# Layer 3's FFN: the last unit's parts between the attention's first steps in the first call, and in two halves of the tokens in the second

## The chip, the cores and the metric

The kernel runs on one core of a Trainium2 chip. The core has five engines with queues of their own: TensorE (PE, with its weight loads as PEld), VectorE (DVE), ScalarE (ACT), GpSimd (POOL) and SyncE (SP, which issues DMAs here). The metric is the device time of one execution in microseconds; the time before is the median of three runs, 2940.64 us.

## The reference

A macaron network of four layers on x, which has 2048 rows of 128. Each layer is an FFN with weight 0.5, an attention, and the same FFN again; each gets the normed x:

```
x = x + 0.5 * L3_ffn(layernorm(x))
x = x +       L3_attn(layernorm(x))
x = x + 0.5 * L3_ffn(layernorm(x))
```

For this case only layer 3 matters. Its attention is dense (16 heads of 8, rotary q and k). Its "FFN" is itself a small transformer of depth 2. One of its layers computes, with h = x whose upper 64 features are shifted by one token:

```
q, k, v = split(h @ wqkv);  q, k normed, scaled, rotated
o = attention in windows of 64 tokens over this and the window before
x = x + o @ wo
h = shift(x);  h = (h - mean) / sqrt(var + 1e-5) * lg + lb
a, g = split(h @ w1 + b1);  x = x + (a * gelu(g)) @ w2 + b2
```

## The kernel before, in words

All arithmetic is in 32-bit floats. x stays in SBUF as 16 tiles of 128 tokens; a *sequence* is four tiles (512 tokens), and there are four. `yT` holds a sequence's normed input with the features on the partitions. The file computes the layers one after the other; at its end stand `l3_ffn(w3, "l3f", True)`, `l3_attn()` and `l3_ffn(w3, "l3g", False)`.

**`l3_ffn` (line 1534 on).** A *unit* is one of the two inner layers for one sequence: eight units, each of four steps (a step is 128 tokens). A loop over steps runs six stages with lags: `project` (p_qk, pv), `to_features`, `weights`, `exponentials`, `turn_weights`, `with_values` (which copies a step's result into `oT`). The rest of a unit is a chain of *parts* over 512 tokens that is placed between later steps by the list `parts`:

- `attended`: pz = oT by wo (four calls), added to yT (L1702), and the shifted copy h (ACT L1551, DVE L1560)
- `mean`: pm, then h - pm (L1711) and its square on ACT
- `variance`: pvar, copied to rs (L1723), and an inverse root of ten small operations on POOL (L184 to L194)
- `spread` and `normed`: dg (L1731), pb = a matmul of dg, h scaled by it (L1741)
- `hidden` for three chunks (128, 128 and 85 columns): two calls into the bank pair pag, gelu on ACT (ge), hh on DVE (L1754)
- `close_unit`: pz2 from hh by w2 (three calls), added to yT (L1766)
- `leave`: transposes back (pt_z), x updated (L1774), and then, in the first call, `leave_normed`, or in the second, the DMA of the sequence to the output

For the last unit no later step is left to stand beside these parts: the loop runs on to `n_steps + 14` with nothing else in it.

**`leave_normed`** makes a *chain* of parts for the next layer: statistics of x on DVE (L202 to L190), scaling to y (L214), the turn to `yT` (pt_y on PE, L241 on ACT). A chain's part runs at a `tick()`, which the loops call after each stage; a tick that is told it is busy, or that has run one part with matmuls, leaves further such parts for later.

**`l3_attn`, `dense_attention` (line 720 on).** Four sequences of four units with four key tiles, in two halves: 128 half-steps. A half-step is scores (pk), the maxima of five steps ahead (pq on PE, L752 on DVE), the exponential on ACT (L787), and the product with the values (po). Before the first pk stand, for sequence 0, the four projections with their evacuations (L1499 and L1505), the sum on POOL (L1506), the marked keys km, the values, and ten maxima.

**What sets the order.** Matmuls, and the operations of ACT that are marked so, stand in the order in which the program emits them. DVE, POOL and SP are ordered by a scheduler among what is emitted. Semaphores come from the use of tiles: a tile of a pool waits until the one that had its place is read.

**PSUM.** There are eight banks of 512 columns. `l3_ffn` has `d=3` pairs (p_qk, pt_qk, ps, pt, pag) and `m=2` single banks for the rest. The attention has `MIX`: one pair k (pk), two pairs q (pq), one bank o (po), one bank m for all else:

```
MIX = dict(k=1, q=2, o=1, m=1)
```

Of the kernel before, what the change touches and what calls it, by code (L numbers as in the profile page):

```python
# [25 lines left out]
ALU = mybir.AluOpType  # L26
AX = mybir.AxisListType

P = 128
# [74 lines left out]
def tile_macaron(ctx, tc, x_in, const_in, vec_in, w0_in, ws_in, ws3_in, w2f_in, w3_in, out):  # L104
# [17 lines left out]
    def bank(tag, name):  # L122
        n = 2 if tag in "kqd" else 1
        return psum["pool"].tile([P, n * 512], F32, tag=tag, name=name, bufs=psum["bufs"][tag])
# [595 lines left out]
    def dense_attention(sb, prepare, finish, wo, masked, tiles=None):  # L720
# [119 lines left out]
        for u, (b, j) in enumerate(units):  # L840
            n = TB * u
            later.setdefault((n - 1, 0), []).append(lambda u=u: queries(u))
            later.setdefault((n + 5, 1), []).append(lambda u=u: end(u))
            if j == 3:
                later.setdefault((n + 6, 1), []).append(lambda b=b: output(b))
                later.setdefault((n + 7, 1), []).append(lambda b=b: project(b))
            if j == 0:
                for at, f in prepare(b, seq(b)["vh"], seq(b)):
                    if b or at >= -LEAD:
                        later.setdefault((n + math.floor(at), int(at % 1 * 2)), []).append(f)  # L850
                    else:
                        f()

        for n in range(-LEAD, n_steps + 5):
            for half in range(2):
# [675 lines left out]

    def l3_ffn(w3, tag, first):
        with pool(tag) as sb, banks(tag + "ps", d=3, m=2):
            units = [(l, b) for l in range(2) for b in range(B)]
            n_steps = TB * len(units)
# [4 lines left out]
                return W3(w3, f"{name}{l}")  # L1542

            def tmp(name):
                return sb.tile([P, S], F32, tag="tmp", name=name, bufs=4)

            def act(*args, **kw):
                tc.keep_in_program_order(nc.scalar.activation(*args, **kw))  # L1548
# [1 line left out]
            def act_copy(dst, src):  # L1550
                tc.keep_in_program_order(nc.scalar.copy(dst, src))  # L1551

            def pair(name):
                return bank("d", name)

            def shift(dst, src):

                act_copy(dst[0:64], src[0:64])
                nc.gpsimd.memset(dst[64:128, 0:1], 0.0)
                nc.vector.tensor_copy(dst[64:128, 1:S], src[64:128, 0 : S - 1])  # L1560

            def norm_unit(u):
                l, b = units[u]
# [113 lines left out]
            def with_values(step):  # L1677
                u, t = step // TB, step % TB
                st = s_state[step]
                PT = st["PT"]  # L1680
                po = bank("m", "po3")
                for fc in range(4):
                    for w, v in enumerate((st["vb"], st["v"])):
                        for r in range(2):
                            h = 2 * fc + r
                            mm_in_order(
                                po[64 * r : 64 * r + 64, fc * P + w * 64 : fc * P + w * 64 + 64],
                                v[:, ts(h, 64)], PT[:, r * 4 + fc, ts(w, 64)],
                            )
                if t == 0:  # L1690
                    u_state[u]["oT"] = sb.tile([P, 4, S], F32, tag="oT", name="oT")
                nc.vector.tensor_copy(u_state[u]["oT"][:, :, ts(t, P)], po.rearrange("p (c n) -> p c n", n=P))
                s_state.pop(step - 1, None)

            def attended(u):
                l, b = units[u]
                oT = u_state[u]["oT"]
                pz = bank("m", "pz")
                for fc in range(4):
                    mm_in_order(pz, W(l, "wo").rearrange("p (c n) -> p c n", n=D)[:, fc, :], oT[:, fc, :], fc == 0, fc == 3)  # L1700
                z = yT[:, b, :]
                nc.vector.tensor_add(z, pz, z)  # L1702
                h2 = sb.tile([P, S], F32, tag="h2", name="h2", bufs=2)
                shift(h2, z)
                u_state[u]["h2"] = h2

            def mean(u):
                h2 = u_state[u]["h2"]
                pm = bank("m", "pm")
                mm_in_order(pm, onesm, h2)  # L1710
                nc.vector.tensor_sub(h2, h2, pm)  # L1711
                sq = tmp("sq2")
                act(sq, h2, AF.Square)
                u_state[u]["sq"] = sq

            def variance(u):

                sq = u_state[u].pop("sq")
                pv = bank("m", "pvar")
                for t in range(TB):  # L1720
                    mm_in_order(pv[:, 2 * t : 2 * t + 2], sq[:, ts(t, P)], onesm[:, 0:2])
                rs = sb.tile([P, TB], F32, tag="rs", name="rs", bufs=2)
                nc.vector.tensor_copy(rs, pv[:, : 2 * TB].rearrange("p (t i) -> p t i", i=2)[:, :, 0])  # L1723
                inverse_root(sb, rs, rs, "ir4", ALU.add, 1e-5, nc.gpsimd)
                u_state[u]["rs"] = rs

            def spread(u):

                rs = u_state[u].pop("rs")
                dg = tmp("dg")  # L1730
                nc.vector.scalar_tensor_tensor(  # L1731
                    dg.rearrange("p (t n) -> p t n", n=P), rows(ident, TB), float(D), bcast(rs, P), ALU.mult, ALU.mult
                )
                u_state[u]["dg"] = dg

            def normed(u):
                l, b = units[u]
                h2 = u_state[u]["h2"]
                pb = bank("m", "pb3")
                mm_in_order(pb, onesm, u_state[u].pop("dg"))  # L1740
                nc.vector.scalar_tensor_tensor(h2, h2, W(l, "lg"), pb, ALU.mult, ALU.mult)  # L1741

            def hidden(u, c):
                l, b = units[u]
                at, n = HCH[c]
                h2, w1 = u_state[u]["h2"], W(l, "w1")
                if c == 0:
                    u_state[u]["hh"] = sb.tile([P, 3, S], F32, tag="hh", name="hh")
                p = pair("pag")
                mm_in_order(p[:n, 0:512], w1[:, HID + at : HID + at + n], h2)  # L1750
                mm_in_order(p[:n, 512:1024], w1[:, at : at + n], h2)
                ge = tmp("ge")
                act(ge[:n, :], p[:n, 0:512], AF.Gelu, bias=W(l, "b1g")[:n, c : c + 1])
                nc.vector.scalar_tensor_tensor(  # L1754
                    u_state[u]["hh"][:n, c, :], p[:n, 512:1024], W(l, "b1a")[:n, c : c + 1], ge[:n, :], ALU.add, ALU.mult
                )

            def close_unit(u):
                l, b = units[u]
                hh = u_state[u]["hh"]  # L1760
                w2 = W(l, "w2").rearrange("p (c n) -> p c n", n=D)
                z = yT[:, b, :]
                pz = bank("m", "pz2")
                for c, (_, n) in enumerate(HCH):
                    mm_in_order(pz, w2[:n, c, :], hh[:n, c, :], c == 0, c == 2)
                nc.vector.scalar_tensor_tensor(z, pz, W(l, "b2"), z, ALU.add, ALU.add)  # L1766
                del u_state[u]

            def leave(b):
                pt = bank("m", "pt_z")  # L1770
                for t in range(TB):
                    transpose_in_order(pt[:, ts(t, P)], yT[:, b, ts(t, P)])
                xb = x[:, ts(b, TB), :].rearrange("p t d -> p (t d)")
                nc.vector.scalar_tensor_tensor(xb, pt, 0.5, xb, ALU.mult, ALU.add)  # L1774
                if first:
                    leave_normed(b, chain(b), 3)
                else:
                    nc.sync.dma_start(out[:, ts(b, TB), :], x[:, ts(b, TB), :])

            if first:  # L1780
                for l in range(2):
# [14 lines left out]
                (lambda u: hidden(u, 0), 12, 5), (lambda u: hidden(u, 1), 13, 0), (lambda u: hidden(u, 2), 13, 0),  # L1796
                (close_unit, 13, 4), (lambda u: leave(units[u][1]) if units[u][0] else None, 14, 0),
            ]
            later = {}
            for u in range(len(units)):  # L1800
                for f, after, place in parts:
                    later.setdefault((u * TB + after, place), []).append((f, u))
                later.setdefault((u * TB - 2, 0), []).append((norm_unit, u))
                later.setdefault((u * TB - 1, 0), []).append((open_unit, u))
            for n in range(-2, n_steps + 14):
                for place, (part, lag) in enumerate((
                    (project, 0), (to_features, 2), (exponentials, 4), (weights, 3), (turn_weights, 5), (with_values, 6)
                )):
                    for f, u in later.pop((n, place), ()):
                        f(u)  # L1810
                    if 0 <= n - lag < n_steps:
                        part(n - lag)
                    tick()
            assert not later, later


    with pool("ws") as wp:
# [9 lines left out]
        with pool("l2x") as l2x:  # L1827
# [14 lines left out]
                l2_attn(v4s)  # L1842
                finish_chains()
            l2_ffn("l2g")
    l3_ffn(w3, "l3f", True)
    l3_attn()
    l3_ffn(w3, "l3g", False)

# [142 lines left out]
```

## Time and profile before

| what | value |
|---|---|
| median of three runs | 2940.64 us (2930.02 to 2940.65) |
| profiled execution, own time | 2936.27 us |
| its span, first to last instruction | 2934.6 us |
| busy PE, DVE, ACT, POOL | 78%, 62%, 42%, 31% of the span |
| mean granted clock of PE | 0.864 |
| HBM traffic | 28 GB/s over the span |

The page's shares are means over the whole kernel, of which layer 3 is some 1235 us (from 1700 to the end). A stage's limit is read in that stage: from the busy time in a stretch, from the timeline (start, duration, engine, line, operation, what goes out and in; in brackets the idle time before it and what ended it), and from the granted clock in a stretch.

### The profile page before, as it was taken

The page shows a single profiled execution, that of the slowest core. Times are in us where ns is not written, and L with a number is a line of the kernel's source. Part 1 is how long each engine was busy: PE and PEld are TensorE (multiplying, and loading weights), DVE is VectorE, ACT ScalarE, POOL GpSimd, SP SyncE. Part 2 cuts the span into 40 slices and gives each one's busy share as a digit, 9 for nine tenths or more (in the row PEclk, how much of TensorE's full clock was granted, in tenths as well). Part 3 has the DMA queues.
Part 4 walks back from the last instruction along what each step waited for, and adds up shares of the span by engine and source line. Part 5 has one row for each costly group of instructions (what it writes and reads, how often), then busy time and mean ns, then how long its engine had stood idle before and what let it go on. Part 6 is the DMA issues. An engine that isn't in the chain of part 4 may idle for free.

```text
span 2934.6 us, 46900 instructions
## 1 busy us (share of the span) xinstructions
PE 2274.4 (78%) x17558; PEld 1179.6 (40%) x17558; DVE 1808.6 (62%) x4776; ACT 1246.5 (42%) x2682; POOL 913.9 (31%) x1700
## 2 busy tenths in 40 slices
PE   4277528888678998958577678988689999689987
PEld 2145213333333333338456545555322222355553
DVE  4656476676576676454564477777356564777763
ACT  3044303433332433314232266776224444467763
POOL 1012012332122222202322387775200000677661
PEclk8588758999887999768777789999779999899998
DMA  3042010000000000008105410000000000100000
GB/s 133 0 152 81 0 58 1 1 1 1 1 1 1 1 1 4 4 7 290 36 13 189 143 30 21 21 21 12 1 1 1 1 1 1 26 23 19 21 21 11
DMA packets 33771, 99.12 MB, mean 34 GB/s; under 512 B 6184, under 2 KB 12072, under 8 KB 33032
## 3 DMA queue, kind: packets, MB, share of 16 engines
q1 hardware_dynamic: 30616, 88.03, 9.2%
q0 software_dynamic: 2496, 5.12, 0.8%
q8 instruction: 138, 2.26, 0.3%
q10 hardware_dynamic: 432, 2.98, 0.3%
q14 instruction: 89, 0.73, 0.1%
HBM read 66.88 MB, written 14.55 MB: 28 GB/s over the span
## 4 chain that ended last, share of the span: by engine, by line
PE 51%; DVE 22%; ACT 10%; POOL 9%; issue 6%; DMA 2%; SPq 0%; POOLq 0%; DVEq 0%; ACTq 0%
PE pk_at L164 10%; PE po_at L164 6%; ACT PT L787 4%; PE pa L164 3%; PE pag L164 3%; PE po L164 3%; PE pe L164 3%; PE p_qk L164 2%; POOL t L1603 2%; PE pg L164 2%; DVE t L1599 2%; PE pv L164 2%; DVE t L1596 2%; DVE y L997 2%; PE pq_at L164 2%
## 5 line engine op out<-in xcount | busy, mean ns | idle before, releaser
L787 ACT ACTIVATE PT<-pk_at 128x1024 f32<-128x1024 f32 (+3 forms) x384 | 311.1, 810 | 554.6 <-PE pq_at L164 478.1
L164 PE MATMUL pk_at<-qx,km 32*128 32x512 f32 (+3 forms) x1536 | 372.2, 562 | 62.3 <-ACT PT L787 57.3
L164 PE MATMUL po_at<-PT,vh 128*32 128x512 f32 (+3 forms) x1536 | 335.1, 519 | 3.1 <-POOL PT L790 2.8
L757 DVE CUSTOM_DVE_ANT_0 s<-pq_at,cst 128x384 f32<-128x384 f32 (+3 forms) x512 | 248.6, 485 | 100.8 <-PE pq_at L164 89.5
L1548 ACT ACTIVATE s<-s,nm,rn 128x128 f32<-128x128 f32 x512 | 245.5, 482 | 2.3 <-DVE nm L1654 2.0
L790 POOL TENSOR_SCALAR_AFFINE_SELECT PT<-PT 128x256 f32<-128x256 f32 x256 | 107.6, 422 | 422.9 <-ACT PT L787 422.8
L164 PE MATMUL pq_at<-km,qT 32*128 32x384 f32 (+3 forms) x1024 | 225.9, 530 | 14.1 <-DVE nm L757 7.7
L164 PEld LDWEIGHTS pk_at<-qx,km 32*128 32x128 f32 x1536 | 121.0, 191 | 271.9 <-ACT PT L787 209.0
L752 DVE TENSOR_REDUCE nm<-pq_at 128x2 f32<-128x1024 f32 x128 | 156.2, 1225 | 104.8 <-PE pq_at L164 104.0
L1603 POOL TENSOR_TENSOR t<-t,t 128x1024 f32<-128x1024 f32 x64 | 151.5, 2367 | 134.7 <-DVE t L1599 134.4
L161 PE MATMUL pt_y<-ident,y 128*128 128x128 f32 x224 | 54.6, 375 | 156.9 <-DVE y L214 117.9
L164 PE MATMUL pq_at<-km,t 32*128 32x512 f32 x512 | 149.6, 690 | 7.0 <-DVE nm L752 4.8
L164 PE MATMUL p_qk<-w,hT 128*128 128x512 f32 x256 | 144.0, 691 | 10.8 <-DVE t L1599 9.0
L164 PEld LDWEIGHTS po_at<-PT,vh 128*32 128x32 f32 x1536 | 56.0, 110 | 222.7 <-issue 148.2
L161 PE MATMUL pt<-ident,s 128*128 128x128 f32 x640 | 93.3, 293 | 65.4 <-POOL s L1666 40.4
L241 ACT COPY yT<-pt_y 128x512 f32<-128x512 f32 x56 | 32.8, 585 | 258.1 <-PE pt_y L161 258.1
L1666 POOL TENSOR_TENSOR s<-s,sm 128x1024 f32<-128x1024 f32 x64 | 121.5, 1898 | 49.1 <-DVE sm L1665 41.0
L1596 DVE TENSOR_TENSOR t<-p_qk,w 128x1024 f32<-128x1024 f32 x64 | 78.3, 1223 | 71.4 <-ACT sq L1548 71.1
L1548 ACT ACTIVATE sq<-p_qk 128x1024 f32<-128x1024 f32 x64 | 65.6, 1024 | 128.3 <-PE p_qk L164 72.7
L161 PEld LDWEIGHTS pt<-ident,s 128*128 128x128 f32 x640 | 78.6, 151 | 97.6 <-POOL s L1666 51.3
L161 PEld LDWEIGHTS pt_y<-ident,y 128*128 128x128 f32 x224 | 34.6, 171 | 188.1 <-issue 112.1
L1290 DVE SCALAR_TENSOR_TENSOR hT<-pa,w,sg 128x128 f32<-128x128 f32 x184 | 51.8, 345 | 85.1 <-ACT sg L1289 64.0
(424 smaller groups left out, 5197.0 us busy)
## 6 DMA issues: line engine op xcount, KB each, us to landing
w<-in_w2f_dram SPq DMA_DIRECT2D x46, 836.0 KB, 5.8
vb<-v SPq DMA_DIRECT2D x112, 128.0 KB, 2.2
skew<-qe SPq DMA_DIRECT2D x16, 512.0 KB, 3.0
rel<-skew SPq DMA_DIRECT2D x64, 128.0 KB, 3.5
w<-in_w_dram SPq DMA_DIRECT2D x1, 4147.0 KB, 12.4
w<-in_w_dram SPq DMA_DIRECT2D x1, 3200.0 KB
od<-o SPq DMA_DIRECT2D x46, 64.0 KB, 4.9
yd<-y SPq DMA_DIRECT2D x8, 256.0 KB, 2.3
```

The source lines that it names most:

```text
L161: return nc.tensor.transpose(dst, src, ident[: src.shape[0], : src.shape[0]])
L164: tc.keep_in_program_order(nc.tensor.matmul(dst, lhsT=lhsT, rhs=rhs, start=start, stop=stop))
L752: nc.vector.tensor_reduce(to, pq.rearrange("p (i n) -> p i n", i=2), AX.X, ALU.max)
L757: nc.vector.tensor_tensor_reduce(s[:, :nk], pq[:, i * 512 : i * 512 + nk], causal[:, S - nk :], 1.0, -BIG, ALU.add, ALU.max, nm[:, qt, at ...
L787: by_order(nc.scalar.activation(PT[:, :, q0:], pk[:, :, q0:], AF.Exp, scale=SC8))
L790: nc.gpsimd.affine_select(d, d, pattern=[[0, 2], [1, P]], base=0, channel_multiplier=-1, compare_op=ALU.is_ge, fill=0.0)
L997: nc.vector.scalar_tensor_tensor(yt, pe[e // 4][:, ts(e % 4, D)], st["g"][:, t, e : e + 1], yt, ALU.mult, ALU.add)
L1548: tc.keep_in_program_order(nc.scalar.activation(*args, **kw))
L1596: nc.vector.tensor_mul(by_head(t1), by_head(p3), over(tab[:, 0]))
L1599: nc.vector.tensor_mul(by_head(t2[:, :, a]), by_head(p3[:, :, z]), over(tab[:, 1, :, a]))
L1603: nc.gpsimd.tensor_add(t1, t1, t2)
L1666: nc.gpsimd.tensor_mul(s, s, bcast(sm, P))
```

## The change

1. A pool `l3r` (`rb`) is opened around both calls and the attention. The tiles of the unit's later parts (tmp, oT, h2, hh, rs and the root's) are in it, so that they outlive the FFN's own pool.
2. In `l3_ffn` the last unit is left out of `parts`, and the loop ends at `n_steps + 7`. Its ten parts are put in the list `rest`. In the first call they become a chain, one part for each tick, that the attention's loop runs. In the second they are run at once, each part for tokens 0 to 255 and then 256 to 511; to that end the parts take a slice `at`.
3. In `dense_attention`, for an attention without a causal mask (layer 3's only), a tick follows each of sequence 0's first preparing steps.
4. `pag` of a part that runs in the attention takes a pair of q instead of d, and all single banks are then the attention's one m.
5. The last unit's inverse root is on DVE (eight operations) instead of POOL.

```diff
@@ dense_attention
                         later.setdefault((n + math.floor(at), int(at % 1 * 2)), []).append(f)
                     else:
                         f()
+                        if not masked:
+                            tick()
@@ l3_ffn
-    def l3_ffn(w3, tag, first):
+    def l3_ffn(w3, tag, first, rb):
...
             def pair(name):
-                return bank("d", name)
+                return bank("d" if "d" in psum["bufs"] else "q", name)
...
-                    u_state[u]["oT"] = sb.tile([P, 4, S], F32, tag="oT", name="oT")
+                    u_state[u]["oT"] = rb.tile([P, 4, S], F32, tag="oT", name="oT")
...
-            def mean(u):
-                h2 = u_state[u]["h2"]
+            def mean(u, at=whole):
+                h2, n = u_state[u]["h2"], at.stop - at.start
                 pm = bank("m", "pm")
-                mm_in_order(pm, onesm, h2)
-                nc.vector.tensor_sub(h2, h2, pm)
-                sq = tmp("sq2")
-                act(sq, h2, AF.Square)
+                mm_in_order(pm[:, :n], onesm, h2[:, at])
+                nc.vector.tensor_sub(h2[:, at], h2[:, at], pm[:, :n])
+                sq = u_state[u]["sq", at.start] = tmp("sq2")
+                act(sq[:, :n], h2[:, at], AF.Square)
...
-                inverse_root(sb, rs, rs, "ir4", ALU.add, 1e-5, nc.gpsimd)
+                eng = nc.vector if u == len(units) - 1 else nc.gpsimd
+                inverse_root(rb, rs[:, :n], rs[:, :n], f"ir{n}", ALU.add, 1e-5, eng)
...
                 else:
-                    nc.sync.dma_start(out[:, ts(b, TB), :], x[:, ts(b, TB), :])
+                    nc.sync.dma_start(out[:, tiles, :], x[:, tiles, :])
...
-            later = {}
+            later, last = {}, len(units) - 1
             for u in range(len(units)):
-                for f, after, place in parts:
+                for f, after, place in parts if u < last else ():
                     later.setdefault((u * TB + after, place), []).append((f, u))
...
-            for n in range(-2, n_steps + 14):
+            for n in range(-2, n_steps + 7):
...
             assert not later, later
+            rest = [attended, mean, variance, spread, normed]
+            rest += [lambda u, at, c=c: hidden(u, c, at) for c in range(3)] + [close_unit, lambda u, at: leave(units[u][1], at)]
+            if first:
+                spare = chain(units[last][1])
+                for f in rest:
+                    spare(1, lambda f=f: f(last, whole), f is not spread)
+            else:
+                for f in rest:
+                    for at in (slice(0, S // 2), slice(S // 2, S)):
+                        f(last, at)
@@ tile_macaron
-    l3_ffn(w3, "l3f", True)
-    l3_attn()
-    l3_ffn(w3, "l3g", False)
+    with pool("l3r") as rb:
+        l3_ffn(w3, "l3f", True, rb)
+        l3_attn()
+        l3_ffn(w3, "l3g", False, rb)
```

## The prediction

> **What bounds the kernel now.** I first read the busy time in stretches that follow the code: the last steps of the first call of layer 3's FFN, the opening of the attention behind it, the attention itself, and the end of the second call.
>
> ```profile
> 2083.70:2120.20 36.50, 22.25 (x50) 9.40 (x50) 15.51 (x53) 4.38 (x7) 6.57 (x16) 0.78 0.00 0
> 2120.20:2153.70 33.50, 25.82 (x62) 9.09 (x66) 15.94 (x17) 1.52 (x2) 2.68 (x3) 0.50 0.00 0
> 2153.70:2460.00 306.30, 281.98 (x1566) 76.56 (x1558) 182.70 (x239) 131.74 (x140) 7.61 (x6) 0.98 0.00 1
> 2903.00:2934.60 31.60, 18.91 (x42) 7.49 (x42) 7.56 (x12) 3.30 (x5) 2.01 (x10) 0.82 0.04 17
> ```
>
> The columns are the stretch, its length, busy time of PE, PEld, DVE, ACT and POOL, PE's granted clock, DMA share and GB/s. The steady attention has PE busy 92% at clock 0.98. The three other stretches (101.6 us) do not: no engine is saturated, and in the second the clock is 0.50 throughout. The timeline says why: the last unit's tail, and then the opening of the attention, are each one chain in which every engine waits for the one before it.
>
> ```profile
> 2083.79 3.70 PE L164 MATMUL pz<-oT,w 128*128 128x512 f32 x8 [0.21 <-DVE oT L1692]
> ...
> 2102.05 7.99 PE L164 MATMUL pag<-h,w 128*128 128x512 f32 x12 [0.92 <-DVE h L1741]
> ...
> 2120.22 2.07 PE L164 MATMUL p<-yT,ws 128*128 128x512 f32 x2 [0.68 <-ACT yT L241]
> 2122.33 0.75 DVE L1499 SCALAR_TENSOR_TENSOR t<-p,ws,cst 128x512 f32<-128x512 f32 x1 [3.32 <-PE p L164]
> 2123.14 2.08 PE L164 MATMUL p<-yT,ws 128*128 128x512 f32 x2 [0.84 <-DVE t L1499]
> ...
> 2153.72 1.06 PE L164 MATMUL pk_at<-qx,km 32*128 32x512 f32 x2
> ```
>
> The tail runs from 2083.8 to 2120.2, and only then comes the first projection of the attention, although its input (sequence 0) has long been normed. The first scores (pk) start at 2153.7. These are the edges between which the change works. The end of the kernel is the same tail once more:
>
> ```profile
> 2902.92 3.70 PE L164 MATMUL pz<-oT,w 128*128 128x512 f32 x8 [0.21 <-DVE oT L1692]
> ...
> 2914.81 0.69 DVE L1731 SCALAR_TENSOR_TENSOR dg<-ident,rs 128x512 f32<-128x512 f32 x1 [2.87 <-POOL rs L194]
> ...
> 2918.55 7.63 PE L164 MATMUL pag<-h,w 128*128 128x512 f32 x12 [0.92 <-DVE h L1741]
> ...
> 2930.46 0.69 DVE L1774 SCALAR_TENSOR_TENSOR x<-pt_z,x 128x512 f32<-128x512 f32 x1 [0.75 <-PE pt_z L161]
> 2931.18 0.33 SPq L1778 DMA_DIRECT2D out_dram<-x  x1
> ```
>
> Nothing lies beside it, so every microsecond cut here is cut from the end.
>
> **The clock decides most prices.** A 512-column call on 128 rows is two instructions. Its pair takes 2.08 us at half clock (the p rows above), about 1.05 at full (pm at 2908.06 took 1.12). Within a run an instruction costs 0.46 at full (pz: 8 in 3.70) and about 0.87 at half (pag at 2102.05: 6 in the 5.2 us up to 2107.26, where the clock rises, then 6 in 2.8). The granted clock changes only at multiples of 3.41 us, so I cut windows at those edges:
>
> ```profile
> 2086.78:2090.19 3.41, 0.80 (x3) 0.12 (x2) 3.03 (x8) 0.62 (x1) 1.27 (x1) 1.00 0.00 0
> 2090.19:2093.60 3.41, 2.72 (x6) 1.18 (x6) 0.69 (x1) 0.65 (x2) 0.00 (x0) 0.50 0.00 0
> ...
> 2124.32:2127.74 3.42, 2.58 (x4) 0.50 (x2) 1.11 (x2) 0.36 (x1) 1.26 (x1) 0.50 0.00 0
> 2127.74:2131.15 3.41, 2.44 (x3) 0.50 (x2) 1.30 (x3) 1.16 (x2) 0.00 (x0) 0.50 0.00 0
> 2694.34:2697.75 3.41, 2.23 (x11) 1.57 (x12) 1.04 (x4) 2.54 (x7) 3.13 (x6) 1.00 0.17 38
> 2697.75:2701.17 3.42, 3.42 (x8) 1.68 (x7) 1.06 (x2) 1.55 (x2) 1.76 (x10) 0.50 0.00 0
> ```
>
> After a window with PE busy 0.80, and even 2.23 of 3.41 us, the next one is at half clock. At half clock 2.58 busy is not enough to leave it, 2.72 is. The Trainium skill ("TensorE: Matmul & The Clock Gate", Part 1, What's actually happening) has the clock fall only after an idle window of about 3.4 us. By that rule the interleaved stretch, whose gaps are all under 2 us, would stay at full clock once pz has raised it, and I would gain some 4 us more than below. The rows say otherwise, and I follow them: a chain of one call (1.05) and one evacuation (0.85) keeps PE busy about 1.9 us per window, so it falls to half clock, and there (2.08 of 2.93, that is 2.4 per window) stays until a long run of matmuls comes.
>
> **First call, part by part.** In the order in which the changed kernel's instructions stand, PE gets: the turn of sequence 2 (pt_y), pz, then in turn projection, pm, projection, pvar, projection, pb, projection, then the three pag parts alternating with the first maxima (pq), and pz2, pt_z and the turn of sequence 3 among the other maxima. No instruction is taken away except POOL's 10 of the inverse root, 2095.46 to 2098.21, which become 8 on DVE. DVE's own inverse root at 2116.30 to 2117.86 prices them at 0.2 each.
>
> *Lost:* pz stood before pt_y, now behind it. Its input y is scaled by 2088.3, pt_y ends at 2088.7, its copy (0.58, ACT L241) frees the single m bank at 2089.3. So pz starts 5.5 us later than before.
>
> *Shared bank:* m has two buffers in the FFN and one in the attention, so each call waits for the evacuation before it. From 2089.35: pz in the mixed clock to 2095.1, z added to 2095.8; projection (1.05) and t (0.75) to 2097.8; pm and its subtraction to 2099.6; projection and t to 2101.5; pvar and rs to 2102.8. Then, at half clock: projection to 2104.9, t to 2105.7, the rest of the root and dg to 2107.4, pb to 2109.5, h to 2110.3, the last projection to 2112.4. Km (POOL 1.26, ACT and DVE) lies beside this.
>
> *pag and pq:* pag's c0 follows without a gap, and projection and c0 together raise the clock, so c0 ends at 2115.0. POOL's sum of q is ready at 2114.5, and the first pq stands to 2116.1. pag has the two buffers of q with the pq between, so c1 waits for c0's hh (to 2116.6) and c2 for c1's (to 2120.1), since the 1.23 us maximum (L752) lies on DVE between them; the last hh ends at 2123.6.
>
> *DVE afterwards:* seven maxima 8.6, vh 0.7, z 0.75, x 0.7, statistics and root of sequence 3 3.2, qx 0.7, y 1.1 make 15.7, then 0.9 for the turn that stands before pk: first pk at 2140.2. Against 2153.7 that is **13.5 us**. The ticks add nothing later: from pk on, the PE order is the old one. In the old trace the attention stayed at half clock until 2165.3, and I take the same number of slow steps after the change.
>
> *At nothing:* The four memsets of vh and nm (2.4 us on POOL) come earlier, as the tail's tiles no longer lie in the pool whose space they take. The new pool needs space, no instruction. SP gets nothing new here.
>
> **Second call, in halves.** 256-column prices are not all in the trace for these lines: L1414 (128x256 from PSUM on DVE) took 417 ns against about 690 for 512, L787 at 128x256 on ACT took 381. From pz at 2902.92: first half to 2904.8, z to 2905.3, h to 2905.8; second half of pz to 2906.7. pm of the first half follows at once, its subtraction ends at 2907.6; DVE has it before the second half's shift, so the second half's subtraction ends at 2908.9 and pvar at 2910.0. DVE interleaves the two roots: dg at 2912.1 and 2913.1 against 2915.5. Then pb twice at half clock to 2914.3 and 24 half-size pag instructions from there without a gap: about 10 at 0.43 and 14 at 0.23, to 2921.7 (before: 2926.2). The end after pag is ge 0.4, hh 0.45, one last pz2 call 0.5, z 0.45, two transposes 0.4, x 0.4: 2924.5, where before it was 2931.15. The last transfer I leave at its 3.4 us (2931.18 to 2934.6). SP issues one more DMA, which comes earlier beside the other half's work. This is **6.7 us**, from 5 (pag cold throughout, 24 at 0.43) to 9 (pag warm).
>
> The sum is 20.2 us: the span 2934.6 becomes 2914.4. The profiled run took 2936.27, the median of the three runs is 2940.64, and the three spread over 10.6 us. From the median I take the same amount: **2920.5**.
>
> **Rivals.**
>
> *Half clock throughout* (pag and pq among each other never warm it, because pq uses 32 rows): window 2148.22 to 2151.63 had only such work, PE fully busy, and stayed at 0.5. Adding the half-clock price at each step above puts pk at about 2158.6, 4.9 later than now; with 6.7 from the end, 1.8 is left: 2938.8. A stretch that is cold in part lies between.
>
> *Warm after pz*, as the skill's rule has it: 6 us more in the opening and 2 at the end, 2912.
>
> *Slower:* the opening all cold, and the half clock carried further into the attention than the present 11.6 us. A step there costs 3.87 (2161.29 to 2165.16) against 2.31 at full clock, 1.6 more. With 1.8 left, two further cold steps turn it slower, ten make 14 us: 2955. Against it: with po in the step one full window sufficed at 2161.87.
>
> *Nothing happens*, because a scheduler restores the old order: excluded by the instruction order.
>
> **How the numbers follow.** About 0.5% (14.7 us) is what a measurement of this kernel can tell from no change. Chances: mixed clock 0.50 (own range 2914 to 2928), warm 0.20, cold or mostly cold 0.25 (2929 to 2940), slower 0.05. Below 2925.9 lie 0.43 of the first, all of the second, 0.02 of the third: faster 0.65, same 0.29, slower 0.06. The range 2909 to 2937 reaches to the warm case less 3 us for the spread of runs and to most of the cold one.
>
> **What would show it.** First pk about 13 us earlier after the leave of unit 6; pz behind pt_y by 5.5; windows at 0.5 around the projections and 1.0 at pag; the end some 25 us after its pz instead of 31.7. Wrong if the clock is 0.5 through pag, if c1 and c2 wait for DVE longer than two maxima, or if the attention's slow steps become more.

## The result, and the profile after

| | before | after |
|---|---|---|
| median, us (11 runs each) | 2935.52 (2926.83 to 2942.72) | 2920.74 (2914.22 to 2927.43) |
| ratio, with its 95% interval | | 0.9945 (0.9932 to 0.9957) |
| profiled execution: its own time / its span | 2936.27 / 2934.6 | 2915.74 / 2914.0 |

The change makes the kernel faster by about 0.55%: by the ratio 16.1 us, between 12.6 and 20.0; the two medians differ by 14.8. The forecast was 2920.5 us, and the median is 2920.74. That agreement is in part luck: the forecast subtracted 20.2 us from a median of three runs, 2940.64, which lies 5.1 us above the median of eleven. The gain was forecast 4 to 5 us too large and the base 5 us too high, and the two errors cancel.

First the windows of the profile after, for the opening (from unit 6's x to the first pk), the attention up to the last pk, and the end from pz. The columns are the stretch, its length, busy time of PE, PEld, DVE, ACT and POOL, PE's granted clock, DMA share and GB/s.

```profile
2078.50:2136.30 57.80, 43.01 (x114) 15.90 (x114) 31.55 (x79) 5.41 (x8) 6.04 (x9) 0.81 0.00 0
2136.30:2478.90 342.60, 317.74 (x1701) 85.04 (x1700) 189.50 (x248) 147.04 (x156) 8.46 (x7) 0.97 0.00 1
2889.30:2914.00 24.70, 17.20 (x72) 13.60 (x72) 11.28 (x39) 4.47 (x10) 0.00 (x0) 0.91 0.06 22
```

Between the same edges the first two stretches of before were these:

```profile
2083.70:2153.70 70.00, 48.07 (x112) 18.49 (x116) 31.45 (x70) 5.90 (x9) 9.25 (x18) 0.64 0.00 0
2153.70:2492.50 338.80, 312.31 (x1702) 83.93 (x1694) 190.16 (x248) 146.59 (x155) 7.61 (x6) 0.98 0.00 1
```

The third, from pz to the end, took 31.7 us at clock 0.82. So the opening and the end became shorter and warmer, and the attention, in which nothing was changed, became 3.8 us longer.

The timeline of the opening after the change; the columns are start, length, engine, line, operation, output<-input, and in brackets the idle time before the instruction and what released it:

```profile
2082.56 1.09 PE L161 MATMUL pt_y<-ident,y 128*128 128x128 f32 x4 [4.12 <-DVE y L214]
2084.33 6.60 PE L164 MATMUL pz<-oT,w 128*128 128x512 f32 x8 [0.68 <-ACT yT L241]
2091.78 1.12 PE L164 MATMUL p<-yT,ws 128*128 128x512 f32 x2 [0.85 <-DVE yT L1716]
2093.91 1.10 PE L164 MATMUL pm<-h,onesm 128*128 128x512 f32 x2 [1.00 <-DVE t L1501]
2095.78 1.12 PE L164 MATMUL p<-yT,ws 128*128 128x512 f32 x2 [0.78 <-DVE h L1725]
...
2102.68 2.07 PE L164 MATMUL pb<-dg,onesm 128*128 128x512 f32 x2 [2.43 <-DVE dg L1744]
2105.67 2.07 PE L164 MATMUL p<-yT,ws 128*128 128x512 f32 x2 [0.92 <-DVE h L1754]
2107.54 3.44 PE L164 MATMUL pag<-h,w 128*128 128x512 f32 x4
...
2112.55 1.98 PE L164 MATMUL pag<-h,w 128*128 128x512 f32 x4 [0.51 <-DVE hh L1767]
2116.09 1.95 PE L164 MATMUL pag<-h,w 128*85 128x512 f32 x4 [0.51 <-DVE hh L1767]
...
2136.28 1.23 PE L164 MATMUL pk_at<-qx,km 32*128 32x512 f32 x2
```

The reader sees the chain that the prediction laid out: pz stands behind the turn pt_y and starts only when ACT has copied pt_y out of the single m bank; projections (p) and the tail's calls take turns; the second and third pag wait for the hh of the part before. And the end, with the same columns:

```profile
2889.30 3.72 PE L164 MATMUL pz<-oT,w 128*128 128x256 f32 x16 [0.21 <-DVE oT L1700]
...
2897.72 0.42 DVE L1744 SCALAR_TENSOR_TENSOR dg<-ident,rs 128x256 f32<-128x256 f32 x1
...
2898.64 0.43 DVE L1744 SCALAR_TENSOR_TENSOR dg<-ident,rs 128x256 f32<-128x256 f32 x1
...
2900.20 6.52 PE L164 MATMUL pag<-h,w 128*128 128x256 f32 x24
...
2910.37 0.42 DVE L1790 SCALAR_TENSOR_TENSOR x<-pt_z,x 128x256 f32<-128x256 f32 x1 [0.20 <-PE pt_z L161]
```

From pz to the end of the last transfer it is now 24.7 us, where it was 31.7.

### The profile page after: what moved, and what is told of

The parts are those of the page before. It is cut to its first block, busy times and chain, and to the rows that moved or that the text cites. A ratio compares the mean times of both kernels' runs of the same rounds, so it can differ in the third digit from the quotient of the medians.

```text
span 2914.0 us, 46993 instructions
## 1 busy us (share of the span) xinstructions
PE 2267.7 (78%) x17588; PEld 1177.3 (40%) x17588; DVE 1814.6 (62%) x4811; ACT 1247.0 (43%) x2687; POOL 907.1 (31%) x1680
## 3 DMA queue, kind: packets, MB, share of 16 engines
q8 instruction: 139, 2.28, 0.3%
```

## The experiments

The theory: the gain is the sum of a shorter opening and a shorter end, the price of each call is set by the clock window that it falls in, and a little is lost again in the attention, because the half and full clock fall differently there. The rival: one of the two parts does all the work, or the clock only accompanies the times and doesn't set them. The table has the stages of each profiled execution, in us: the opening from the start of unit 6's x to the first pk; the attention from the first to the last pk, and in brackets how much of it lies in half-clock windows; the end from the start of the last copy of oT to the end of the last update of x (the last transfer, 3.2 to 3.4 us more, is left out). The ratio is to the kernel before, from all runs of each. The stages are those of one execution each: e3 runs the parts of before in before's order up to its second FFN call, and yet its opening is 1.3 us shorter and its attention 2.1 longer. A difference of 2 us between two profiles carries little.

| kernel | opening | attention (half clock) | end | ratio (95%) |
|---|---|---|---|---|
| before | 70.1 | 338.4 (11.6) | 29.0 | |
| after | 57.8 | 342.2 (22.2) | 22.2 | 0.9945 (0.9932 to 0.9957) |
| e1, as after | 57.8 | 342.2 (22.2) | 23.1 | 0.9953 (0.9936 to 0.9969) |
| e2, opening only | 59.4 | 342.2 (22.2) | 30.0 | 0.9976 (0.9964 to 0.9989) |
| e3, halves only | 68.8 | 340.5 (17.3) | 22.7 | 0.9961 (0.9949 to 0.9974) |
| e4, pz ahead | 52.8 | 339.7 (16.9) | 22.7 | 0.9935 (0.9921 to 0.9948) |
| e5, one matmul more | 59.5 | 338.5 (12.0) | 22.3 | 0.9940 (0.9925 to 0.9956) |
| e6, o bank | 52.0 | 339.6 (16.9) | 22.2 | 0.9904 (0.9888 to 0.9920) |
| e7, statistics late | 55.9 | 340.1 (17.2) | 23.2 | 0.9931 (0.9915 to 0.9948) |
| e8, fill | 63.2 | 336.8 (6.8) | 22.2 | 0.9951 (0.9936 to 0.9966) |
| e9, e4+e6+e7 | 46.1 | 337.9 (11.7) | 22.7 | 0.9881 (0.9860 to 0.9902) |
| e10, e9 with fill | 47.5 | 336.5 (6.8) | 23.1 | 0.9895 (0.9876 to 0.9914) |
| e11, root on POOL | 57.6 | 337.5 (11.4) | 25.0 | 0.9942 (0.9920 to 0.9964) |

**e1: the changed kernel again.** No edit; it runs beside e2 to e4, so that these have it on the same chip.

> The changed kernel itself once more, so that its gain is known as well as that of its parts. Theory (two places add up, each as priced: 12 to 13.5 us in the attention's opening, 7 at the end): 19 to 20 us below before, ratio 0.9935. Rival (part of the 20.6 us between the two profiled spans is the clock's luck, and something in between is lost again): 13 to 16 us, ratio 0.995. First pk 54 us after sequence 2's scaling, 24.7 us from the last unit's pz to the end.

Measured: 2918.54 against 2935.08 us, 16.5 us less by the medians and 13.8 (9.1 to 18.8) by the ratio, as the rival had it. The three stages of the profile are the same as after's within 0.9 us. So the change gives 14 to 17 us and not the 20.2 of the forecast, which lies outside both intervals; something is lost between the two parts, and the table shows where: 3.8 us in the attention.

**e2: the first call's part alone.** The second call's tail stays whole, with its inverse root on POOL.

```diff
-                eng = nc.vector if u == len(units) - 1 else nc.gpsimd
+                eng = nc.vector if first and u == len(units) - 1 else nc.gpsimd
...
-                    for at in (slice(0, S // 2), slice(S // 2, S)):
-                        f(last, at)
+                    f(last, whole)
```

> The first call as changed, the second call's last unit whole and its root on POOL, as before. Theory (two separate places): the end takes 31.7 us from pz again, the opening keeps its 12 to 13 us; ratio 0.9957. Rival (the opening only trades one wait for another, the end carries the gain): ratio 0.999 or more.

Measured: 2926.84 against 2935.08, a gain of 8.2 us by the medians and 7.0 (3.2 to 10.6) by the ratio. That is less than the theory's 0.9957, and more than the rival allowed. The stages say 10.7 from the opening and 3.8 back in the attention: the attention's loss is there too with the end as before.

**e3: the second call's halves alone.** The first call's last unit runs at its old place with its root on POOL, and the ticks between the attention's first steps are gone.

```diff
-                        if not masked:
-                            tick()
...
-                eng = nc.vector if u == len(units) - 1 else nc.gpsimd
+                eng = nc.vector if not first and u == len(units) - 1 else nc.gpsimd
...
-                for f, after, place in parts if u < last else ():
+                for f, after, place in parts if first or u < last else ():
...
-            for n in range(-2, n_steps + 7):
+            for n in range(-2, n_steps + (14 if first else 7)):
...
-            if first:
-                spare = chain(units[last][1])
...
-            else:
+            if not first:
```

> The second call in halves with its root on DVE, the first call's tail and the attention's opening as before. Theory (two separate places): 24.7 us from pz to the end, 7 less; opening 66.5 us from sequence 2's scaling to the first pk as before; ratio 0.9976. Rival (the halves save nothing, since PE's matmuls of pag bound the end): ratio 1.000.

Measured: 2925.35 against 2935.08, 9.7 us less by the medians and 11.4 (7.6 to 15.0) by the ratio, more than the 7 us expected. The end is 6.3 shorter. The steps of the second FFN call, which no edit touches, were 3.6 us shorter in this profiled execution (391.7 against 395.3), with 34 us of them at half clock where before has 44. So the halves, with their root on DVE, are worth 6 to 7 us, as forecast; that the rest is clock windows that fell well fits this one execution and is not shown for the others. Both parts are needed: on the same chip the mean of e1's runs lies 7.1 us below e2's and 5.6 below e3's, with standard errors of 2.5 and 2.2, so the rival that one does it all is out.

**e4: pz ahead of the attention.** The tail's first part stands again before the attention's turn pt_y; the rest stays between its steps.

```diff
-                for f, after, place in parts if u < last else ():
+                for f, after, place in parts if u < last else parts[:1] if first else ():
...
-                for f in rest:
+                for f in rest[1:]:
```

> As changed, but the last unit's first part (pz, the sum, the shifted copy) stays at its old place, ahead of the turn of sequence 2, in the FFN's two single banks. Theory (the step called lost: pz behind pt_y costs 5.5 us of the chain): first pk 5 to 7 us earlier than in the changed kernel, 48 us after sequence 2's scaling; ratio 0.992. Rival (the maxima on DVE bound the opening, so what comes earlier waits there): first pk less than 2 us earlier.

Measured: the opening is 52.8 us, 5.0 less than after, beside the 5.5 that the prediction charged for pz behind pt_y. pz now also runs warm:

```profile
2079.78 3.70 PE L164 MATMUL pz<-oT,w 128*128 128x512 f32 x8 [0.21 <-DVE oT L1700]
...
2083.70 1.01 PE L161 MATMUL pt_y<-ident,y 128*128 128x128 f32 x4 [0.22 <-DVE y L214]
```

It takes 3.70 us where after's pz took 6.60, with pt_y behind it at no cost, since y comes at that time anyhow. Counted from x, pz starts 5.7 us earlier and ends 8.6 earlier than in after. Of these, 5.0 reach the first pk: its first two projections ran at half clock (2.07 and 2.08 us, where after's took 1.12).

**e5: one matmul more, in the middle of the attention.** A 512-column product whose result nobody reads, before half-step 30, to move what follows against the clock's windows.

```diff
                 tick(bool(fs))
                 for f in fs:
                     f()
+                if not masked and (n, half) == (30, 0):
+                    mm_in_order(bank("m", "pf"), ident, cst[:, :512])
```

> As changed, with one idle matmul more (128 by 512, into the bank m, never read, some 0.93 us at full clock) in the attention's step 30. It leaves nothing out. Theory (after the change the attention's second change of sequence falls just behind an edge of the clock's 3.41 us windows, which costs a stretch at half clock at 206.5 us behind the first pk, about 4.4 us): moved by 0.93 us it does not fill a window, no half clock there, and the attention from first to last pk takes 339 us instead of 342.2, though it does more. Rival (the half clock there comes from the work itself, that is from sequence 3's later preparation): half clock as before, attention 343.1.

Measured: with a matmul more, the attention is 338.5 us long, 3.7 less than after and as expected. These are the windows of after around the place where the sequence changes; the columns are those of the windows above.

```profile
2339.37:2342.78 3.41, 2.21 (x10) 0.57 (x8) 2.46 (x4) 3.37 (x4) 0.91 (x1) 1.00 0.00 0
2342.78:2346.19 3.41, 3.41 (x9) 0.26 (x7) 2.03 (x2) 0.00 (x0) 0.00 (x0) 0.50 0.00 0
2346.19:2349.61 3.42, 2.65 (x8) 1.17 (x6) 0.55 (x2) 0.00 (x0) 0.00 (x0) 0.50 0.00 0
2349.61:2353.02 3.41, 3.41 (x13) 0.70 (x12) 1.58 (x2) 0.83 (x1) 0.00 (x0) 0.50 0.00 0
```

At the change of sequence PE has a gap, and the gap fell so that one window held only 2.21 us of PE work; three windows at half clock follow. In e5 the change of sequence falls 0.7 us later in its window, so the gap is shared by two windows, and the clock stays full there. The third row is e5's whole attention:

```profile
2342.22:2345.63 3.41, 2.65 (x16) 0.44 (x8) 2.19 (x5) 2.77 (x4) 1.27 (x1) 1.00 0.00 0
2345.63:2349.04 3.41, 2.70 (x12) 0.86 (x12) 2.98 (x4) 0.68 (x1) 0.00 (x0) 1.00 0.00 0
2139.06:2478.02 338.96, 314.35 (x1703) 84.56 (x1702) 189.61 (x248) 147.03 (x156) 8.47 (x7) 0.98 0.00 1
```

The clock there is 0.98 where after has 0.97, and PE's busy time is 3.4 us less for more instructions. The added work was expected to remove the stretch, and it did; this speaks for the clock as what sets the time, and not the reverse. Its runs' ratio, 0.9940, can't be told from e1's; the 3.7 us is the profiled execution's.

The phase is not mere chance. In after, e1 and e2 the first pk came at 2136.28, 2139.48 and 2138.09, but each time 1.65 to 1.71 us into its window, and each of the three has the second stretch. Other openings have other phases: 2.24 in e11, 0.16 in e4.

**e6: a bank of their own for the tail's calls.** In the attention pz, pm, pvar, pb, pz2 and pt_z take an o bank, not yet in use there, in place of the single m bank.

```diff
+            def lone(name):
+                return bank("o" if "o" in psum["bufs"] else "m", name)
...
-                pz = bank("m", "pz")
+                pz = lone("pz")
```

(and so for the other five)

> As changed, but the last unit's single banks in the attention are the bank o, which is free until the first po, so that its parts and the projections no longer take turns on the one bank m. Theory (the shared bank costs one evacuation, 0.7 to 0.85 us, at each of four turns): opening 3 to 4 us shorter than 57.8, 54.5. Rival (the chain of dependences is what each call waits for, not the bank): less than 1 us shorter.

Measured: the opening is 52.0, 5.8 less than after and more than was expected; the median is 2911.89 against 2943.19. The timeline shows both effects: a projection follows pz without a gap, and pm needs not wait for its evacuation. The opening's half-clock time fell too, from 22.2 to 17.3 us, so the clock has a share in the 5.8.

```profile
2087.97 6.16 PE L164 MATMUL pz<-oT,w 128*128 128x512 f32 x8 [0.67 <-ACT yT L241]
2093.97 1.02 PE L164 MATMUL p<-yT,ws 128*128 128x512 f32 x2
2095.64 1.13 PE L164 MATMUL pm<-h,onesm 128*128 128x512 f32 x2 [0.64 <-ACT h L1557]
```

**e7: the statistics of sequence 3 later.** Behind the tail the statistics, the root and the scaling of sequence 3 lie among the maxima that the first pk waits for. They wait 30 ticks here.

```diff
-    def leave_normed(b, spare, gap):
+    def leave_normed(b, spare, gap, start=1):
...
-        spare(1, lambda: st.append(statistics(x, b)), False)
+        spare(start, lambda: st.append(statistics(x, b, None, start > 1)), False)
...
-                    leave_normed(b, chain(b), 3)
+                    leave_normed(b, chain(b), 3, 30 if "o" in psum["bufs"] else 1)
```

> As changed, but the statistics, the scaling and the turn of sequence 3 come 30 ticks later (its first is held in order; the scheduler still puts three of the statistics early). Theory (behind the last hh DVE bounds the opening, where these stand between the maxima): first pk 3 us earlier, opening 54.8. Rival (the maxima wait for PE and the small operations fill gaps): less than 1 us.

Measured: the opening is 55.9, 1.9 less than after, between the two expectations. Some of the statistics' instructions still stand among the maxima; the eight of the root (0.16 each) and the scaling (1.11) are gone, 2.4 us of DVE, which agrees with the 1.9.

**e8: the chain kept warm.** Calls of 256 columns that nobody reads, between the attention's first steps, so that PE is busy in every window.

```diff
+        def fill(n):
+            if not masked:
+                pf = bank("o", "pf")
+                for _ in range(n):
+                    mm_in_order(pf[:, :256], ident, cst[:, :256])
...
+                            fill(2)
                             tick()
+                            fill(2)
...
+                if n < 0:
+                    fill(1)
                 tick(bool(fs))
                 for f in fs:
                     f()
+                if n < 0:
+                    fill(1)
```

> As changed, with idle matmuls (128 by 256, into the bank o, never read, two instructions of 0.23 us at full clock each) before and after each tick of the attention's opening, two in its first part, one from the maxima on. It leaves nothing out. Theory (the half clock sets the prices of pb, the last projection, pag's first chunk and the first steps of the attention): the opening's 22 us at half clock shrink below 10, opening 2 us shorter, and the attention's first 12 us at half clock go, 3 us more. Rival (the idle calls stand in the way of the real ones, each by up to its own length): opening 3 us longer or more.

Measured: the clock does what was meant. Half-clock windows in the opening fall from 22.2 us to 6.8, and those in the attention too (by the same two figures). The opening is all the same 5.4 us longer than after, and the attention 5.4 shorter.

```profile
2084.00:2150.00 66.00, 60.65 (x243) 31.62 (x242) 34.50 (x80) 6.71 (x10) 7.34 (x9) 0.95 0.00 1
```

PE is now busy 60.65 of 66.0 us: the fill stands in PE's order ahead of calls that are ready.

```profile
2106.91 3.49 PE L164 MATMUL pf<-cst,ident 128*128 128x256 f32 x12
...
2112.10 1.12 PE L164 MATMUL pb<-dg,onesm 128*128 128x512 f32 x2
```

The warm clock nearly halves the price of a call in the chain (pb 1.12 us, where after has 2.07), but the fill calls cost the opening more than that saved, and the attention gave back as much. For the opening alone the rival won.

**e9: e4, e6 and e7 together.**

> As changed, with the three edits that shortened the opening by themselves put together: pz at its old place (5.0 us there), the last unit's single banks in the bank o (5.7), sequence 3's statistics later (1.8). Theory (each takes another part of the chain): the opening from 57.8 to 45 or 46 us; the attention between 338.4 and 342.2 by where its changes of sequence fall among the clock's windows; ratio 0.988 to 0.990. Rival (pz earlier and the free bank shorten the same stretch up to the last hh): opening 50 or more, ratio no better than the 0.9904 of the bank o alone.

Measured: 2902.04 against 2933.23 us, ratio 0.9881. The opening is 46.1, near the sum of the three gains (57.8 less 5.0, 5.8 and 1.9 is 45.1). This version beats the changed kernel by 0.6% and the one before by 1.2%; it is the best found, though its interval overlaps e6's and e10's; from e6 it is told apart by the opening in the profile, 46.1 against 52.0.

```profile
2080.46 3.70 PE L164 MATMUL pz<-oT,w 128*128 128x512 f32 x8 [0.21 <-DVE oT L1700]
...
2126.40 1.06 PE L164 MATMUL pk_at<-qx,km 32*128 32x512 f32 x2
```

**e10: e9 with fill in the last steps before the attention's first pk.** Four calls of 512 columns that nobody reads, in a k bank, to meet only the half clock of the attention's first 12 us.

```diff
+                if -2 <= n < 0 and not masked:
+                    mm_in_order(bank("k", "pf")[:, :512], ident, cst[:, :512])
```

> The combination, with four idle matmuls (128 by 512, into the pair k ahead of the first pk, never read), one in each of the last four half-steps before the first pk. It leaves nothing out. Theory (PE is idle enough there, as DVE's maxima bound it, and matmuls on all rows raise the clock): opening at most 2 us longer, and the attention's first 12 us at half clock shrink by half or more, 2 to 5 us less; together 1 to 3 us less. Rival (they stand in the way as the idle matmuls of the whole opening did): 1 to 3 us more.

Measured: opening 1.4 longer, attention 1.4 shorter, median 2902.96 against e9's 2902.04. The half clock of the first 12 us is gone, but a stretch of 6.8 us appeared behind the first change of sequence, 116 us into the attention, where e4, e6 and e7 have one too. Nothing is gained.

**e11: the last unit's root on POOL.** The changed kernel with the root at its old engine, in both calls.

```diff
-                eng = nc.vector if u == len(units) - 1 else nc.gpsimd
+                eng = nc.gpsimd
```

> As changed, but the last unit's inverse roots stay on POOL in both calls. Theory (on DVE the second half's root no longer stands behind the first half's ten operations of 0.28 us): at the end the second half's dg comes 2 to 3 us later and the end takes 1 to 2 us longer (24 instead of 22.2 from the last oT); in the opening, where the root waits for a projection's t on DVE, less than 1 us either way. Rival (the root is hidden there too): the end as changed within 0.5 us.

Measured: the end is 25.0, 2.8 longer than after; the opening is the same (57.6): dg starts 23.4 us behind x in both, as on DVE the root stands among km and t.

```profile
2891.66 0.43 DVE L1744 SCALAR_TENSOR_TENSOR dg<-ident,rs 128x256 f32<-128x256 f32 x1 [2.10 <-POOL rs L194]
...
2893.56 0.43 DVE L1744 SCALAR_TENSOR_TENSOR dg<-ident,rs 128x256 f32<-128x256 f32 x1 [1.47 <-POOL rs L194]
...
2895.11 7.13 PE L164 MATMUL pag<-h,w 128*128 128x256 f32 x24
```

Both dg wait for POOL, and pag takes 7.13 us where after has 6.52, as more of it falls into half clock. So of the end's 6.8 us (29.0 to 22.2) the halves without the engine change give about 4. The attention of this execution is 337.5, with no second half-clock stretch, and by the ratio e11 can't be told from after although its end is longer. So the loss in the attention goes with the phase and not with the interleaving as such; its mean over the runs stays unknown.

## Why the prediction was right, and where it was not

The stretch ahead of the change was 5.1 us shorter in the profiled execution after than before, so 5.1 is added to after's times to set them against the forecast's. (In the thirteen profiles unit 6's x comes anywhere from 2075.4 to 2090.9.)

| step | forecast | measured |
|---|---|---|
| pz starts | 2089.35 | 2089.5 |
| z added | 2095.8 | 2096.9 |
| second projection's t done | 2101.5 | 2102.8 |
| dg done | 2107.4 | 2107.8 |
| last projection done | 2112.4 | 2112.9 |
| pag c0 done | 2115.0 | 2116.1 |
| last hh | 2123.6 | 2124.8 |
| first pk | 2140.2 | 2141.4 |
| end, from its pz: the two dg | 9.2, 10.2 | 8.8, 9.8 |
| end: pag, from and to | 11.4, 18.8 | 10.9, 17.4 |
| end: last x; all done | 21.6; 25.0 | 21.5; 24.7 |

*pz behind pt_y* was right in place and price: a delay of 5.5 us was forecast and 5.7 measured, and e4 gets 5.0 back. The miss is its clock: pz ran at half clock for longer than the mixed price assumed, 6.60 us instead of 5.75, which is most of the 1.1 us that the chain carries on.

*The shared bank* was right: up to the last projection every call in after's timeline waits for the evacuation named for it (pb for its own dg), and e6, which frees them, saves 5.8, part of it by the clock.

*The clock by rows, not by the rule.* These are after's windows through the projections:

```profile
2090.20:2093.61 3.41, 1.85 (x4) 0.30 (x2) 1.72 (x3) 0.62 (x1) 0.00 (x0) 1.00 0.00 0
2093.61:2097.02 3.41, 2.22 (x4) 0.59 (x4) 0.91 (x3) 0.63 (x1) 0.00 (x0) 1.00 0.00 0
2097.03:2100.44 3.41, 2.15 (x10) 1.26 (x10) 2.17 (x8) 1.30 (x2) 1.26 (x1) 1.00 0.00 0
2100.44:2103.85 3.41, 1.17 (x2) 0.50 (x2) 2.01 (x7) 0.22 (x1) 0.00 (x0) 0.50 0.00 0
2103.85:2107.26 3.41, 2.49 (x4) 0.83 (x3) 0.75 (x1) 0.00 (x0) 0.00 (x0) 0.50 0.00 0
2107.27:2110.68 3.41, 3.41 (x5) 1.01 (x3) 0.75 (x1) 0.00 (x0) 1.26 (x1) 0.50 0.00 0
2110.68:2114.09 3.41, 2.90 (x9) 0.98 (x8) 1.88 (x2) 0.69 (x1) 0.00 (x0) 1.00 0.00 0
```

After a window with PE busy 2.15 of 3.41 us the clock fell, and 2.49 did not raise it. The Trainium skill ("TensorE: Matmul & The Clock Gate", Part 1, What's actually happening) has it fall after an idle window; here PE was never idle for one, and it fell, so the measurement decides. The warm rival, 2912, is thereby out (the prediction gives it 4 us in one place, and 6 and 2 in another; 2912 is from the second).

But the forecast's own rule, that a chain with PE busy about 1.9 us per window falls to half clock, is not right either. The window at 2090.20 with 1.85 busy and the next with 2.22 kept the full clock, and only the third lost it. The trace of before could have told: from 1990 us on it has seven full-clock windows with 1.7 to 2.1 us busy, and six of them kept it. So the rule doesn't explain the fall, although a fall among the projections was what the forecast had. Its place was missed by one projection: the forecast had the third projection at half clock, and it ran at full (1.13), while pag c0, which it had warmed by the end, ran at half throughout (3.44). These two nearly cancel. The cold rival is out too: c1 and c2 ran at full (1.98 and 1.95).

The "half clock throughout" rival rests on a window, 2148.22 to 2151.63, that had 0.82 us of the turn pm_at on 128 rows besides pq on 32, so it did not have "only such work"; the last section shows that its point about 32 rows holds.

*The end* came to 7.0 us where 6.7 was forecast. pag began 0.5 earlier and was 0.9 shorter than its 7.4 (6.52), with more of it warm, but the parts behind it took 4.1 us where 2.8 was forecast; these misses nearly cancel. e3 and e11 confirm the halves and the root as the causes.

*The step that failed* is the sentence "I take the same number of slow steps after the change". The first 12 us behind pk were as slow as before (12.0 and 11.6 us at half clock). But the attention has 338 us more in which the clock can fall, and with the new opening its phase against the windows was another: a second half-clock stretch of 10.24 us, from 2342.78 on, came with the loss of 3.8. The sum by the measured terms is 12.3 + 7.0 − 3.8 = 15.5, where the forecast had 13.5 + 6.7 = 20.2; the ratio says 16.1. The prediction itself lists it as a sign of being wrong that "the attention's slow steps become more", and they did. It was not as the slower rival had it, though: the half clock behind the first pk went no further than before, the new stretch lies 206.5 us behind the first pk, and it is worth 3.8 us and not the 14 of ten cold steps.

What stays open is how often the second stretch occurs over the executions of one kernel, and what holds the phase of an opening so steady. after, e1 and e2 have the stretch in the same place, e5 and e11 not at all, and only one execution of each was profiled.

## What to carry to other kernels

A chain in which every engine waits for the one before can be hidden by putting another such chain between its steps, but then look for what the two now share: here one PSUM bank and the order of pz and pt_y cost 5.8 and 5.0 us, nearly the 12.3 that the interleaving saved in the opening. Price the calls by the clock of the window that they fall in, and count also the later stages, whose phase against the clock's windows an edit ahead of them can move. Filling the clock's idle windows with work that nobody reads did not pay in either of the two kernels that tried it (e8 and e10): what the clock gave, the calls that stood behind the fill lost.

## What was not expected of the hardware

The attention, with the same work (save for e5's matmul, and sequence 3's turn in e7, e9 and e10), took 336.5 to 342.2 us, and its length went with where its gaps fell in the 3.41 us windows. Take the update of x at a change of sequence as a mark. The second one comes 194 to 199 us behind the first pk. Where it fell 0.18 to 0.20 us into a window (after, e1, e2), a half-clock stretch of 10.2 us followed; at 0.45 to 1.28 us (e11, e6, e9, e4, e10, e7, e5, before), none; at 3.02 and 3.23 (e3, e8), one of 3.4 us. At the first change of sequence, 105 to 110 us in, 2.38 to 2.44 gave 6.8 us (e4, e6, e7, e10), 2.99 gave 3.4 (e8), and 0.80 to 2.18 none (the other eight). In e5 an added matmul thus went with a shorter time.

Nor was it expected that PE's busy time in a window would tell so little of the next window's clock. At the same gap a window with 2.21 us lost the full clock in after and kept it in e11. Over the 11031 windows of all thirteen traces, no full-clock window with less than 1.41 us busy kept the clock, and none with more than 3.03 lost it, but in between both happened: of 428 windows with 2.1 to 2.3 us busy, 319 kept it. At half clock, none with less than 2.68 us raised it.

Part of the rest is the shape of the calls. From 1990 us on the thirteen traces have 206 half-clock windows in which PE was busy for 3.35 us or more. The 166 without any matmul on 32 rows all raised the clock; of the 14 with 2.28 us or more of such matmuls (pq and pk) none did, and of the 26 between 18.
